# Neighbour quantiles over 16 graphs: the 21-slot end block sorted in mid-round, a later read-back, last finishes side by side, and the second round's tiles sorted entry by entry

## The chip, the cores and the metric

The kernel runs on one core of one Trainium2 chip. The metric is device microseconds of one execution. Timed runs of the kernel before, three of them, have a median of 7,337.73 us (7,328.73 to 7,385.34). One execution was also taken with the hardware profiler; it has its own time, which is given below.

## The reference

The input is a batch of B = 16 graphs ("entries") of N = 1024 nodes with C = 64 features, and a dense weighted adjacency that has about 16 neighbours in a row. Four layers follow each other, each with a residual and a layernorm. Layers 0 and 1 are dense products with the adjacency and small matrices. Layers 2 and 3 ("layer 0" and "layer 1" of the kernel's quantile part) drop some neighbours, and then take for each node and each feature a weighted sum of three quantiles over the neighbours that are left:

```python
adj_d = _dilate_adj(adj, mask)
# per node and feature: sort the valid neighbours' values, interpolate
sv = jnp.sort(jnp.where(valid[..., None], x[:, None, :, :], big), axis=2)
for tau, wt in zip((0.25, 0.5, 0.75), (0.25, 0.5, 0.25)):
    pos = jnp.clip(tau * (mf - 1.0), 0.0)
    lo, hi = floor(pos), ceil(pos)
    agg = agg + wt * (gather(lo) * (1.0 - frac) + gather(hi) * frac)
out = x + agg
y = relu(out @ W1 + b1) @ W2 + b2
x = _layernorm(x + y * mask)
```

The neighbour lists are the same in both quantile layers; the values are not.

## The kernel before

**Tiles and sizes.** The nodes of an entry are ordered by their number of neighbours and cut into NT = 8 tiles of 128. Tile t has lists of SIZES[t] slots (10, 11, 13, 14, 15, 17 and 19 for tiles 0 to 6). A slot of a tile is a [128, 64] fp32 block: one neighbour of each of 128 nodes. The eighth tile is split in two halves of 64 nodes, with 21 and 33 slots; the even and the odd entry of a pair put their halves into the same two blocks, so that each of the two end blocks (plans 7 and 8) is full. "Pair" means two entries that are sorted at once.

**Where the values come from.** Tiles 0 to 6 are gathered: `fetch_one` issues one indirect DMA per slot and entry on the GpSimd queue (L378), from a table in HBM into a ring `got_s` of ROOM = 60 slots by two entries. A tile takes SIZES[t] slots of the ring, and the slots come free when the tile that held them has been sorted and weighed. The end blocks are not gathered: `fill` picks their rows with matmuls. For each of slots 1 to 32 it builds a one-hot matrix `hot` from `place` (three of four on VectorE, one of four in two steps on ScalarE), runs 24 matmuls with it into PSUM (`pick`, L374), and after each four slots ScalarE copies them to the end blocks `got` (L780).

**Sorting and weighing.** `exchange` runs a pruned merge-exchange network on VectorE, with min and max between the tile and a scratch tile `other`. All VectorE work that is recorded through the `Metered` wrapper has line L211 in the profile. `weigh` then multiplies the wanted slots on ScalarE (L829 for tiles, L820 for end blocks) and adds them on VectorE into `agg`.

**Rounds.** The 16 rounds are quantile layer and pair: (0,0), (0,1), (1,0), (0,2), (1,1), ... (0,7), (1,6), (1,7). `sort_round(k)` starts the generator `fill(k)`, sorts tiles 6 down to 0 in turn, then waits until the fill is complete and sorts end block 7 (21 slots) and end block 8 (33 slots). In the very first round the two entries of the pair are sorted one after the other (`present` is (0,) and then (1,)); in all others both at once. After a round `finish` runs for its two entries: the small MLP, the layernorm, and 8 row scatters on the GpSimd queue (L888), to the table of the next layer or to the output. After the first quantile layer, `read_back` loads the table again (`x3`, L902 on the SP queue) and splits it into three bf16 parts for the picking matmuls of the second.

**What sets the order.** Nearly everything other than the sorts is a generator: `features` (layers 0 and 1, with `adj_r` loads, L433, on the SP queue), `lists` and `ordered` (which neighbours, and in which order), `fill`, `weigh`, `finish` and `read_back`. A planner, `Weave`, keeps a clock that adds up the estimated VectorE time of what was recorded; each `yield u` of a generator puts its next step u us later on that clock. After each exchange instruction `catch_up` records the steps that are due, and `fetch` issues the gathers for which the ring has room. `advance` and `finish` of the planner jump ahead when there is nothing else to do. VectorE, ScalarE and TensorE keep the recorded order; the GpSimd and SP queues are ordered by the scheduler. Each engine runs its queue in order, and waits for semaphores.

These lines carry the points that the change touches:

```python
for present in ((0,), (1,)) if k == 0 else ((0, 1),):
    tasks += [(k, t, present) for t in reversed(range(LISTED))]
...
weave.finish(filling)
for t in range(LISTED, NS):
    off = sum(SIZES[LISTED:t])
    got = tails[k][:, off : off + SIZES[t], :]
...
    exchange(t, (got, other[:, : SIZES[t], :]), cut)
    summed(t, got, None, (0, 1))
```

Of the kernel before, what the change touches and what calls it, by code (L numbers as in the profile page):

```python
# [26 lines left out]
LEAST = (1,) + SIZES[:7] + (20,)  # L27
# [189 lines left out]
def adj_resnorm_kernel(ctx: ExitStack, tc: tile.TileContext, x, adj_t, nodemask, w01, b01, w02, b02,  # L217
# [49 lines left out]
    def halves_of(b):  # L267

        return (7, 8) if b % 2 == 0 else (8, 7)
# [100 lines left out]
    def pick(dst, hot, parts, first=True):  # L370

        for c in range(NT):
            for q in range(3):
                nc.tensor.matmul(dst, hot[:, c, :], parts[:, c, q, :], start=first and c + q == 0,  # L374
                                 stop=c == NT - 1 and q == 2)
# [386 lines left out]
    def fill(k):  # L762

        while k and (k - 1, NS - 1) not in free:
            yield 1
        size, short = SIZES[NS - 1], SIZES[NS - 2]
        got = tails[k] = s.lists.tile([P, short + size, C], F32, name="got", tag="got_l", bufs=1)
        layer, both = members(k)
        for m, b, e in both:
            while e.parts[layer] is None or e.xs[layer] is None or e.place is None or e.none is None:  # L770
                yield 1
            at = [(rows, (0, short)[plan - LISTED], SIZES[plan]) for rows, plan in zip((lower, upper), halves_of(b))]
            for rows, off, _ in at:
                nc.scalar.copy(got[rows, off, :], e.xs[layer][rows, NT - 1, :])
            waiting = None

            def empty():
                for rows, off, most in at:
                    if waiting[0] < most:
                        nc.scalar.copy(got[rows, off + waiting[0] : off + waiting[0] + 4, :], waiting[1][rows])  # L780

            for i in range(1, size):
                if i % 4 == 1:
                    first, pg = i, pgs[i // 4 % 2]
                if i % 4 == 1:

                    far = s.work.tile([P, NT, P], F16, name="far", bufs=1)
                    nc.scalar.activation(far, e.place, AF.Abs, bias=minus_k[:, i + 2 : i + 3])
                    by_act = s.lists.tile([P, NT, P], BF, name="hot", bufs=HOTS)
                    nc.scalar.activation(by_act, far, AF.Relu, bias=one_f, scale=-1.0)  # L790
                if i % 4 == 3:
                    hot = by_act
                else:
                    hot = s.lists.tile([P, NT, P], BF, name="hot", bufs=HOTS)
                    dve.tensor_scalar(hot, e.place, float(i), None, op0=ALU.is_equal)
                whole = i < LEAST[NS - 2]
                if not whole:
                    nc.tensor.matmul(pg[:, i - first, :], e.none,
                                     ident_b[: KW - 1, i - 1 : i].to_broadcast([KW - 1, C]), start=True, stop=False)
                pick(pg[:, i - first, :], hot, e.parts[layer], whole)  # L800
                yield 2.4
                if i % 4 == 2 and waiting:
                    empty()
                if i % 4 == 0:
                    waiting = first, pg
            yield 5
            empty()
            yield 0.5
            e.filled[layer] = True

    def weigh(k, t, got, agg, which, present):

# [84 lines left out]
    def read_back(b, e, src):  # L897

        while b >= 2 and not entries[b - 2].filled[1]:
            yield 2  # L900
        x3 = s.feat.tile([P, NT, C], F32, name="x3", bufs=1)
        nc.sync.dma_start(x3, src[:N, :].rearrange("(t p) c -> p t c", p=P))  # L902
        yield 60
        parts = s.feat.tile([P, NT, 3, C], BF, name="x3p", bufs=2)
        yield from split(x3, parts, x3)
        e.parts[1] = parts
# [43 lines left out]
    tails = {}  # L950
# [5 lines left out]
    order_of_rounds += [(1, B // 2 - 2), (1, B // 2 - 1)]  # L956
    tasks = []
    for k in range(len(order_of_rounds)):
        for present in ((0,), (1,)) if k == 0 else ((0, 1),):
            tasks += [(k, t, present) for t in reversed(range(LISTED))]  # L960

    def prepare():
# [55 lines left out]
    def finish_round(k, agg, sums):  # L1018
        for gen in sums:
            while weave.runs(gen):  # L1020
                yield 1
        layer, both = members(k)
        if k == len(order_of_rounds) - 1:
            for m, b, e in both:
                weave.add(finish(b, e, layer, agg[:, m], m == 1))
            return
        for m, b, e in both:
            yield from finish(b, e, layer, agg[:, m])

    def exchange(t, pair, view):  # L1030

# [6 lines left out]
    def sort_round(k):  # L1038

        if k >= 2:  # L1040
            weave.finish(rounds[k - 2])
        filling = weave.add(fill(k), 4.0, 0.7 if k < 3 else 1.0)
        agg = s.feat.tile([P, 2, NT, C], F32, name="agg")
        sums = []

        def summed(t, got, which, present):
            if len(sums) >= 2:
                weave.finish(sums[-2])
            sums.append(weave.add(weigh(k, t, got, agg, which, present)))
            weave.catch_up()  # L1050

        for n, (_, t, present) in enumerate(tasks):
            if tasks[n][0] != k:
                continue
            fetch(n)
            got = gots[n]
            which = slice(present[0], present[-1] + 1)
            count = len(present)
            other = s.lists.tile([P, WIDE, C], F32, name="other", bufs=1)
            other = other[:, : count * SIZES[t], :].rearrange("p (e s) c -> p e s c", e=count)  # L1060
            exchange(t, (got[:, which], other), cut_pair)
# [319 lines left out]
```

## Time and profile before

| | |
|---|---|
| median of three timed runs | 7,337.73 us (7,328.73 to 7,385.34) |
| time of the profiled execution | 5,306.79 us |
| its span, first to last instruction | 5,304.9 us |
| mean granted TensorE clock | 0.743 |
| VectorE (DVE) busy | 4,297.6 us, 9,266 instructions |
| GpSimd (POOL) busy | 3,464.7 us, of it 3,170.9 in 2,944 gathers |
| TensorE (PE) busy | 3,435.2 us, 43,576 matmuls |
| ScalarE (ACT) busy | 2,809.1 us, 6,314 instructions |
| HBM traffic | 239.37 MB read, 12.59 MB written |

The profiled execution was 2,031 us shorter than the median of the timed runs. All durations of single instructions below are from the profiled execution. "Busy" is the time in which an engine executes; time in which its queue waits for a semaphore or spends on issuing is not in it. A wait is put down to what ended it: "DVE other <- DMA got_s" is time in which VectorE stood ahead of an instruction that writes `other`, until a gather into `got_s` had landed. The matmul durations overlap each other, so that the sum of their means is more than the busy time.

### The profile page before, as it was taken

The numbers are of one execution on the slowest core, as the hardware profiler recorded it, in microseconds if no ns is written. First come the engines' busy times: TensorE is split into PE (matmuls) and PEld (weight loads), VectorE is DVE, ScalarE is ACT, GpSimd is POOL, SyncE is SP. The second block draws the span as 40 slices with busy tenths as digits, with TensorE's granted clock in tenths as the row PEclk, the third lists the DMA queues.
The fourth block names the chain that finished last, engine by engine and source line by source line (L and its number), as shares of the span: only waits on it lengthen the run. The fifth ranks groups of instructions, "written<-read, shape, count | busy, mean of one in ns | idle before, by whom it ended". The sixth has DMA issues, their size and how long they took to land. (4 is left out here: it accounts for less than half of the span.)

```text
span 5304.9 us, 109613 instructions
## 1 busy us (share of the span) xinstructions
PE 3435.2 (65%) x43576; PEld 2659.3 (50%) x43576; DVE 4297.6 (81%) x9266; ACT 2809.1 (53%) x6314; POOL 3464.7 (65%) x3296
## 2 busy tenths in 40 slices
PE   6878886385775776666776785777769563424152
PEld 5756555264554565555565563655547352324141
DVE  2577849698788989797997988798999999596775
ACT  3466465456564665737384563738475653334242
POOL 0336417757567776767767574776767777777771
PEclk7888787687877787868787786878887775555555
DMA  2212212222222222222212122222222111111110
GB/s 84 76 50 69 68 32 66 47 48 54 48 60 52 59 61 57 57 55 45 73 41 58 46 52 53 57 59 50 60 50 58 25 28 26 25 24 27 26 24 7
DMA packets 420617, 259.31 MB, mean 49 GB/s; under 512 B 106602, under 2 KB 368890, under 8 KB 420090
## 3 DMA queue, kind: packets, MB, share of 16 engines
q0 software_dynamic: 102400, 105.06, 10.4%
q1 hardware_dynamic: 317690, 147.12, 9.7%
q8 instruction: 343, 5.62, 0.5%
q14 instruction: 184, 1.51, 0.1%
HBM read 239.37 MB, written 12.59 MB: 47 GB/s over the span
## 5 line engine op out<-in xcount | busy, mean ns | idle before, releaser
L378 POOL DMA_INDIRECT got_s<-table,idx x2944 | 3170.9, 1077 | 1650.7 <-issue 604.9
L374 PEld LDWEIGHTS <-hot 128*128 128x128 bf16 x24576 | 972.2, 109 | 1011.9 <-DVE hot L211 696.7
L374 PE MATMUL pgk<-x3p,hot 128*128 128x64 bf16 x12288 | 544.0, 211 | 460.8 <-DVE hot L211 396.6
L211 DVE TENSOR_TENSOR other<-got_s 128x512 f32<-128x512 f32 (+9 forms) x850 | 508.7, 609 | 387.4 <-DMA got_s<-table,idx 352.9
L374 PE MATMUL pgk<-x2p,hot 128*128 128x64 bf16 x12288 | 525.5, 208 | 320.4 <-DVE hot L211 261.6
L780 ACT COPY got<-pgk 64x256 f32<-64x256 f32 x416 | 151.6, 365 | 675.8 <-PE pgk L374 670.3
L536 PE MATMUL pr<-steps,near 128*128 128x512 bf16 x1536 | 415.1, 431 | 131.6 <-ACT junk L542 84.6
L211 DVE TENSOR_TENSOR got_s<-got_s 128x128 f32<-128x128 f32 (+9 forms) x867 | 482.0, 560 | 17.8
L481 PE MATMUL pa<-x,adj_r 128*128 128x65 f32 x2048 | 391.3, 375 | 133.7 <-ACT x L404 58.6
L628 PE MATMUL pk<-near,order 128*128 128x512 f16 x2048 | 468.0, 382 | 4.5 <-DVE order L211 4.2
L829 ACT ACTIVATE got_s<-got_s,wts 128x64 f32<-128x64 f32 x1568 | 396.5, 335 | 135.1 <-DVE got_s L211 128.9
L481 PEld LDWEIGHTS pa<-x,adj_r 128*128 128x128 f32 x2048 | 380.6, 289 | 141.7 <-ACT x L404 60.5
L211 DVE TENSOR_TENSOR got_s<-other 128x512 f32<-128x512 f32 (+9 forms) x731 | 402.2, 563 | 7.5
L211 DVE TENSOR_SCALAR hot<-place 128x1024 bf16<-128x1024 f16 x768 | 329.8, 435 | 60.1 <-PE pgk L374 60.0
L536 PEld LDWEIGHTS <-near 128*128 128x128 f16 x1536 | 162.2, 109 | 353.0 <-issue 228.4
L211 DVE TENSOR_TENSOR other<-other 128x384 f32<-128x384 f32 (+10 forms) x617 | 324.0, 525 | 17.3
L211 DVE MAX8 best<-code 128x8 f16<-128x1024 f16 x240 | 293.9, 1225 | 48.1 <-ACT code L639 43.0
L628 PEld LDWEIGHTS <-order 128*128 128x128 bf16 x2048 | 194.0, 98 | 233.6 <-issue 10.6
L542 ACT ACTIVATE junk<-pr,nb_st 128x1024 f16<-128x1024 f32 x256 | 281.7, 1105 | 36.7 <-PE pr L536 35.9
L580 PE MATMUL pv<-minus_n,takes 128*128 128x128 bf16 x1024 | 212.5, 241 | 133.1 <-DVE takes L211 132.6
L790 ACT ACTIVATE hot<-far,one_f 128x1024 bf16<-128x1024 f16 x256 | 294.0, 1148 | 8.6
L450 PE MATMUL px<-adj_r,x_s 128*64 128x128 f32 x2048 | 287.9, 302 | 13.6 <-ACT node_in L453 9.2
(205 smaller groups left out, 6748.9 us busy)
## 6 DMA issues: line engine op xcount, KB each, us to landing
adj_r<-in_adj_dram SPq DMA_DIRECT2D x256, 512.0 KB
got_s<-table,idx POOLq DMA_INDIRECT x2944
x_s<-in_x_dram SPq DMA_DIRECT2D x16, 256.0 KB
table<-x SPq DMA_DIRECT2D x16, 256.0 KB
x<-table SPq DMA_DIRECT2D x16, 256.0 KB
table<-x3s,rows POOLq DMA_INDIRECT x128
out_dram<-agg,out_rows POOLq DMA_INDIRECT x128
table<-no_row SPq DMA_DIRECT2D x12, 0.2 KB
```

The source lines that it names most:

```text
L211: return call(*args, **kwargs)
L374: nc.tensor.matmul(dst, hot[:, c, :], parts[:, c, q, :], start=first and c + q == 0, stop=c == NT - 1 and q == 2)
L378: nc.gpsimd.indirect_dma_start(out=dst, out_offset=None, in_=tab, in_offset=bass.IndirectOffsetOnAxis(ap=rows, axis=0))
L450: nc.tensor.matmul(px[C:, q * P : (q + 1) * P], x_s[:, jt, :], adj[t][:, jt, :], start=jt == 0, stop=jt == NT - 1)
L481: nc.tensor.matmul(pa[:, q, :], adj[i][:, jt, :], x1[:, jt, :], start=jt == 0, stop=jt == NT - 1)
L536: nc.tensor.matmul(pr[:, h * HALF : (h + 1) * HALF], near[:, c, t * P : (t + 1) * P], steps[:, ONSET + h * HALF - c * P :][:, :HALF], star ...
L542: nc.scalar.activation(junk, prs[t - 1], AF.Sign, bias=lim[:, i, t - 1 : t], scale=-1.0, accum_out=cut_at[:, i, t - 1 : t])
L580: nc.tensor.matmul(pv[:, cols], takes[:, c, rows], minus_n, start=False, stop=False)
L628: nc.tensor.matmul(cols, order[:, c, t * P : (t + 1) * P], left(c, slice(h * G, (h + 1) * G)), start=c == 0, stop=c == NT - 1)
L780: nc.scalar.copy(got[rows, off + waiting[0] : off + waiting[0] + 4, :], waiting[1][rows])
L790: nc.scalar.activation(by_act, far, AF.Relu, bias=one_f, scale=-1.0)
L829: nc.scalar.activation(got[:, m, i, :], got[:, m, slot_id, :], AF.Copy, scale=e.wts[:, t, i : i + 1])
```

## The change

`fill` makes two tiles in place of one, of 21 and of 33 slots, and fills in two passes: slots 1 to 20 for both entries, then slots 21 to 32 for both; `filled` notes that a pass is complete. From the third round on, the 21-slot block is sorted and weighed between tile 2 and tile 1 (`end(NS - 2)`), after the planner has recorded the first pass in full; the 33-slot block stays at the end. In the first two rounds both stay at the end. The second round's tiles are sorted one entry after the other, as those of the first were. `read_back` puts 60 us on the planner's clock ahead of its load for entries 0 to 11, and 40 instead of 60 behind it. `finish` of the two entries of a pair runs side by side in the last three rounds, where it did so in the last round alone; the second of the two uses other PSUM banks (`spare`).

```diff
@@ fill
-        size, short = SIZES[NS - 1], SIZES[NS - 2]
-        got = tails[k] = s.lists.tile([P, short + size, C], F32, name="got", tag="got_l", bufs=1)
+        middle, most = SIZES[NS - 2], SIZES[NS - 1]
+        ends = [s.lists.tile([P, size, C], F32, name="got", tag=f"got_{size}", bufs=1) for size in (middle, most)]
+        tails[k] = ends
         layer, both = members(k)
-        for m, b, e in both:
...
-            for i in range(1, size):
-                if i % 4 == 1:
-                    first, pg = i, pgs[i // 4 % 2]
...
-            e.filled[layer] = True
+        groups = 0
+        for low, high in ((1, middle), (middle, most)):
+            for m, b, e in both:
...
+                for i in range(low, high):
+                    if i % 4 == 1:
+                        first, pg = i, pgs[groups % 2]
+                        groups += 1
...
+                yield 5
+                empty()
+                yield 0.5
+                if high == most:
+                    e.filled[layer] = True
+            filled.add((k, low))
@@ read_back
         while b >= 2 and not entries[b - 2].filled[1]:
             yield 2
+        if b < B - 4:
+            yield 60
         x3 = s.feat.tile([P, NT, C], F32, name="x3", bufs=1)
         nc.sync.dma_start(x3, src[:N, :].rearrange("(t p) c -> p t c", p=P))
-        yield 60
+        yield 60 if b >= B - 4 else 40
@@ tasks
-        for present in ((0,), (1,)) if k == 0 else ((0, 1),):
+        for present in ((0,), (1,)) if k < 2 else ((0, 1),):
@@ finish_round
-        if k == len(order_of_rounds) - 1:
+        if k < order_of_rounds.index((0, B // 2 - 1)):
             for m, b, e in both:
-                weave.add(finish(b, e, layer, agg[:, m], m == 1))
-            return
-        for m, b, e in both:
-            yield from finish(b, e, layer, agg[:, m])
+                yield from finish(b, e, layer, agg[:, m])
+        else:
+            ends = [weave.add(finish(b, e, layer, agg[:, m], m == 1)) for m, b, e in both]
+            while any(weave.runs(gen) for gen in ends):
+                yield 1
@@ sort_round
+        def end(t):
+            got = tails[k][t - LISTED]
+            other = s.lists.tile([P, WIDE, C], F32, name="other", bufs=1)
+            exchange(t, (got, other[:, : SIZES[t], :]), cut)
+            summed(t, got, None, (0, 1))
+
         for n, (_, t, present) in enumerate(tasks):
             if tasks[n][0] != k:
                 continue
+            if t == 1 and len(present) == 2:
+                while (k, 1) not in filled:
+                    weave.advance()
+                end(NS - 2)
             fetch(n)
...
         weave.finish(filling)
-        for t in range(LISTED, NS):
-            off = sum(SIZES[LISTED:t])
-            got = tails[k][:, off : off + SIZES[t], :]
-            other = s.lists.tile([P, WIDE, C], F32, name="other", bufs=1)
-            exchange(t, (got, other[:, : SIZES[t], :]), cut)
-            summed(t, got, None, (0, 1))
+        if k < 2:
+            end(NS - 2)
+        end(NS - 1)
```

More of the change, by code (lines that the diff above doesn't have):

```diff
@@ L765, in fill @@
             yield 1
-        size, short = SIZES[NS - 1], SIZES[NS - 2]
-        got = tails[k] = s.lists.tile([P, short + size, C], F32, name="got", tag="got_l", bufs=1)
+        middle, most = SIZES[NS - 2], SIZES[NS - 1]
+        ends = [s.lists.tile([P, size, C], F32, name="got", tag=f"got_{size}", bufs=1) for size in (middle, most)]
+        tails[k] = ends
         layer, both = members(k)
-        for m, b, e in both:
[L770 to L780, printed above, removed]
-            for i in range(1, size):
-                if i % 4 == 1:
-                    first, pg = i, pgs[i // 4 % 2]
[L785 to L808, printed above, removed]
-            e.filled[layer] = True
@@ new lines, in fill, with empty @@
+        groups = 0
+        for low, high in ((1, middle), (middle, most)):
+            for m, b, e in both:
+                while e.parts[layer] is None or e.xs[layer] is None or e.place is None or e.none is None:
+                    yield 1
+                at = [(rows, ends[plan - LISTED], SIZES[plan]) for rows, plan in zip((lower, upper), halves_of(b))]
+                if low == 1:
+                    for rows, got, _ in at:
+                        nc.scalar.copy(got[rows, 0, :], e.xs[layer][rows, NT - 1, :])
+                waiting = None
+                def empty():
+                    for rows, got, size in at:
+                        if waiting[0] < size:
+                            nc.scalar.copy(got[rows, waiting[0] : waiting[0] + 4, :], waiting[1][rows])
+                for i in range(low, high):
+                    if i % 4 == 1:
+                        first, pg = i, pgs[groups % 2]
+                        groups += 1
+                        far = s.work.tile([P, NT, P], F16, name="far", bufs=1)
+                        nc.scalar.activation(far, e.place, AF.Abs, bias=minus_k[:, i + 2 : i + 3])
+                        by_act = s.lists.tile([P, NT, P], BF, name="hot", bufs=HOTS)
+                        nc.scalar.activation(by_act, far, AF.Relu, bias=one_f, scale=-1.0)
+                    if i % 4 == 3:
+                        hot = by_act
+                    else:
+                        hot = s.lists.tile([P, NT, P], BF, name="hot", bufs=HOTS)
+                        dve.tensor_scalar(hot, e.place, float(i), None, op0=ALU.is_equal)
+                    whole = i < LEAST[NS - 2]
+                    if not whole:
+                        nc.tensor.matmul(pg[:, i - first, :], e.none,
+                                         ident_b[: KW - 1, i - 1 : i].to_broadcast([KW - 1, C]), start=True, stop=False)
+                    pick(pg[:, i - first, :], hot, e.parts[layer], whole)
+                    yield 2.4
+                    if i % 4 == 2 and waiting:
+                        empty()
+                    if i % 4 == 0:
+                        waiting = first, pg
+                yield 5
+                empty()
+                yield 0.5
+                if high == most:
+                    e.filled[layer] = True
+            filled.add((k, low))
@@ L949, in adj_resnorm_kernel @@
     weave = Weave()
-    tails = {}
+    tails, filled = {}, set()
     free, gots, room, holders = set(), [], [0], [None] * ROOM
@@ L1022, in finish_round @@
         layer, both = members(k)
-        if k == len(order_of_rounds) - 1:
+        if k < order_of_rounds.index((0, B // 2 - 1)):
             for m, b, e in both:
-                weave.add(finish(b, e, layer, agg[:, m], m == 1))
-            return
-        for m, b, e in both:
-            yield from finish(b, e, layer, agg[:, m])
+                yield from finish(b, e, layer, agg[:, m])
+        else:
+            ends = [weave.add(finish(b, e, layer, agg[:, m], m == 1)) for m, b, e in both]
+            while any(weave.runs(gen) for gen in ends):
+                yield 1
     def exchange(t, pair, view):
```

## The prediction

> **What bounds the kernel now.** First the busy shares and the 40 slices of the page:
>
> ```profile
> PE 3435.2 (65%) x43576; PEld 2659.3 (50%) x43576; DVE 4297.6 (81%) x9266; ACT 2809.1 (53%) x6314; POOL 3464.7 (65%) x3296
> DVE  2577849698788989797997988798999999596775
> POOL 0336417757567776767767574776767777777771
> ```
>
> Two engines share the bound. VectorE (DVE) sorts; GpSimd (POOL) issues the 2,944 row gathers and 256 row scatters. POOL's digit 7 is nearly full: from 4,193 to 5,163 us it issued 696 DMAs in 970 us, 1.39 us each, of which only 1.08 is counted busy and the rest is "issue". So I read the idle time of both, by what ended it: the waits of DVE, then of POOL, then of SP and ACT.
>
> ```profile
> DVE other L211 <- DMA got_s<-table,idx: 352.9, 28, 26.4
> ...
> DVE near L211 <- DMA adj_r<-in_adj_dram: 36.0, 7, 22.6
> ```
> ```profile
> POOL got_s L378 <- DVE idx L211: 310.9, 8, 179.5
> POOL got_s L378 <- DVE other L211: 271.4, 103, 49.6
> ...
> POOL got_s L378 <- DVE y_x L211: 126.4, 3, 125.8
> ```
>
> DVE's great wait is for gathers. POOL's are for neighbour lists (`idx`, start-up) and for ring space (`other`: the sort of a tile must end before its slots are refilled). I then cut the span into rounds; a round begins where DVE starts on the 19-slot tile. Round 7 (2,642 to 2,955 us) shows the pattern:
>
> ```profile
> DVE other L211 <- DMA got_s<-table,idx: 29.2, 2, 24.9
> ...
> POOL got_s L378 <- DVE other L211: 30.6, 7, 28.8
> ```
> ```profile
> 2642.00:2955.00 313.00, 217.82 (x2805) 170.54 (x2805) 267.41 (x566) 175.26 (x402) 216.69 (x202) 0.75 0.22 53
> 4424.00:4699.00 275.00, 105.35 (x1620) 89.36 (x1620) 209.49 (x437) 96.12 (x251) 214.66 (x199) 0.55 0.13 26
> ```
>
> (Columns: window, then PE, PEld, DVE, ACT, POOL busy, clock, DMA.) While DVE sorts the two end blocks at the end of a round, POOL fills the 60-slot ring with the next round's first three tiles and stops (28.8 us). It resumes when the 19-slot tile is sorted, and later DVE stands still until the gathers of tile 1 have landed (24.9 us at 2,812). Both stalls belong to one loop: tail sorts late, ring refilled late, tile 1 late. In rounds 12 to 14 POOL no longer stops, and the round is as long as its 199 or so DMAs.
>
> **What the Trainium skill says.** "VectorE: DVE Perf Modes", section on the TRN2 errata, gives an fp32 tensor_tensor as (N+151)/0.96 ns: 691 ns for 512 elements. The trace has 690, and 286 for 128, so an added instruction costs about 0.15 us beside its elements. "SBUF — State Buffer", section "Who interferes with whom", says that a tensor_tensor with two SBUF inputs takes only a read interface from GpSimd and should not hold up descriptor generation. The trace agrees: a gather has a mean of 1.08 us both in round 7 (216.69/202, DVE 85% busy) and in round 13 (214.66/199, DVE 76% busy). So DVE work moved into a gather wait should not lengthen the wait. "Perfetto Trace Analysis", "Identifying Performance Opportunities", names repeated bubbles on the busiest engine as a sign of too few buffers; here the bubble is that of the ring, which the change leaves at 60 slots.
>
> **The change part by part**, against the profiled execution (5,306.8 us, span 5,304.9).
>
> *1. The 21-slot block moves from the round's end to ahead of tile 1 (rounds 2 to 15).* Its 49 instructions take 20 us: 1,315 to 1,336 in round 2, 5,189 to 5,208 in round 15; none is added. The wait just ahead of tile 1 was, from the timeline, 9.9, 11.8, 10.0, 14.7, 21.8, 24.9, 15.5, 18.0, 8.2 us in rounds 2 to 10 and none in rounds 11 and 12 (round 11 waits 9.1 us ahead of tile 2). The block covers at most 20 of each: 9.9+11.8+10.0+14.7+20+20+15.5+18.0+8.2 = 128 us. Above that stand two floors for rounds 3 to 11 (2,718 us together): DVE has 2,393 busy plus 18 per round of small gaps, 2,555; POOL has 1,797 DMAs at 1.39, 2,498. 2,718 less 118 (rounds 3 to 10) is 2,600, above both but near, so some of the wait will turn up elsewhere, as at tile 2. I take 105; bounds 0 and 128. In rounds 13 to 15 POOL is the limit, so their 142 us of DVE waits stay.
>
> *2. The fill in two passes that this needs.* Slots 1 to 20 of both entries, then 21 to 32 of both: the same 64 hots, 1,536 pairs of weight load and matmul and 26 copies per round, other order. The block's first instruction now waits for the last copy of pass one. Queued behind it on DVE are tile 1, tile 0, the hots of pass two, and so PE and POOL's ring. In the recorded order of after, pass one is complete 10 to 28 us of DVE work before the block in rounds 4 to 12, and just in time in rounds 13 to 15, where DVE waits for gathers anyway. Before, a tail recorded with no such lead (round 5) began without a wait. Cost taken: 0; if the lead is not enough, w us per round, priced below. The two tiles hold the same 54 slots, and the next fill still waits for the 33-slot block.
>
> *3. Last round.* POOL's last gather is at 5,154; tile 1 runs 5,147 to 5,162, tile 0 to 5,176, then finish work, the 21-slot block to 5,208, the 33-slot block to 5,244, `finish` and scatters to 5,305. With the block started at 5,144, tiles 1 and 0 end about 16 us later, at 5,192, the 33-slot sort at 5,228: 16 us gained; bounds 0 and 20.
>
> *4. Round 1 entry by entry.* 222 more DVE instructions: one entry's seven tiles cost 81 us (round 0), two at once 130 (round 1), so 162-130 = 32 us more. But POOL stands 125.8 us at 644 to 769 with the ring full and entry 3 not listed, and from 673 to 808 DVE has 55.7 busy of 135. Entry 2's remaining 44 gathers (44 x 1.29 = 57 us; 1.08 busy and 604.9/2,944 = 0.21 of issue each) and its 81 us of sorts fit there. After 808 DVE has 49 us less to sort and POOL 57 us less to issue. Part is lost to the in-round chain and to entry 5's list, for which POOL waits 42 us at 1,354: I take 35; bounds -32 and 57.
>
> *5. Read back later (entries 0 to 11).* The load `x<-table` is issued 60 us later and the split 40 later:
>
> ```profile
> SPq L902 <- DMA table<-x3s,rows: 1289.3, 15, 431.5
> ```
>
> SP stands in this load until the scatters have landed, with `adj_r` loads queued behind. This reached DVE once, 22.6 us at 3,241. I take 10; bounds 0 and 23. The later split is hidden by the round that lies between layer 1's write and its use (except pair 0, where it lands inside round 2).
>
> *6. `finish` side by side for rounds 13 and 14.* The same operations in parallel banks. Round 13's scatters for entries 14 and 15 come together rather than 70 us apart (4,857 and 4,953), but POOL was busy through that stretch: 0. Round 14's `finish` ends before the end counts: 0.
>
> Sum: 105+16+35+10 = 166 us, 3.1% of the profiled execution: 5,141.
>
> **From there to the timed runs.** Their median, 7,337.7, lies 2,031 us above the profiled execution, and no view shows where. I carry microseconds, not the ratio (which would give 7,108), because the gains are waits of fixed size: 7,337.7 - 166 = 7,172, said as 7,170. A measurement of this kernel can tell about 1% (73 us) from no change.
>
> **Rivals.**
> - *POOL alone is the bound in the timed runs.* If the 2,031 us are slower DMAs (2,031/3,200 = 0.63 us each), POOL never stops, and filling DVE's waits gains nothing. Left are parts 3 and 4: 51 to 73 us, 7,265 to 7,287, within 1%. For it: rounds 12 to 14 already look so. Against it: in the profile POOL stops in each of rounds 3 to 10. The same number results if the waits saved ahead of tile 1 reappear ahead of tile 2 or 0.
> - *The mid-round block waits for its fill: slower.*
>
> ```profile
> ACT got L780 <- PE pgk L374: 670.3, 148, 26.4
> ```
>
>   ACT stands up to 26.4 us for the picking matmuls before it can copy. At the end of a round this had long passed; mid-round DVE would stand w us in each of 14 rounds. The gain is gone at w = 166/14 = 12 us, 1% is lost from (166+73)/14 = 17 us, and 20 us would give 7,337.7+280-166 = 7,452. For it: if PE is what is slower in the timed runs, pass one is late. Against it: the mean of that wait is 4.5 us, and the lead is 10 to 28.
>
> **How the numbers follow.** Forecast 0.62, POOL alone or waits that only move 0.22, fill late 0.16. Prediction 7,170. The low end takes all upper bounds (128+20+57+23 = 228) with the ratio, 7,337.7 x (1-228/5,307) = 7,022, of which I keep 7,050; the high end reaches 50 us into the slower case, 7,390. The forecast's own range is 7,050 to 7,264. Faster by over 1%: 0.62; within 1%: 0.22; slower by over 1%: 0.16.
>
> **What would show it.** Right: DVE's wait for `got_s` falls by about 100 us and POOL's for `other` with it; rounds 4 to 10 shorten by 8 to 20 us; a 20 us run of `got` sorts stands ahead of tile 1; POOL's 125.8 us wait at 644 shrinks to about 70; after the last gather some 133 us remain instead of 150. Wrong: DVE waits for ACT `got` L780's copies at the block, round lengths unchanged with the waits now at tiles 2 and 0, or a profiled gain that the timed runs don't show.

## The result, and the profile after

The changed kernel takes 7,306.04 us (median of 20 timed runs, 7,271.8 to 7,324.09), the kernel before 7,331.09 us (median of 20, 7,301.86 to 7,385.34) beside it. The ratio is 0.9954, with a 95% interval from 0.9938 to 0.9970: 25 us between the medians, and 22 to 45 by the interval. The forecast was 166 us less. On the five chips of e1 to e17 (the "quick chips") the kernel before takes 5,294 to 5,307 us, on the chip of e18 (the "slow chip") 7,348 us, so times are compared only between runs of one chip, or as ratios to the kernel before.

By its span (5,304.9 us) the profile of before is an execution as on a quick chip, and the timed runs are all as on the slow one. On which chips they were made is not known. Only one set of experiments (e18) met the slow chip, so whether the slowness belongs to the chip or to its condition at that time is not shown. The profile of the changed kernel is of the slow kind: its span is 7,299.2 us. Its page:

```profile
PE 3976.7 (54%) x43576; PEld 2896.5 (40%) x43576; DVE 4336.7 (59%) x9509; ACT 2809.6 (38%) x6312; POOL 3320.8 (45%) x3296
...
DVE  2546535757556566465574856557484765647475
...
POOL 0432244444463553525445454546445353665652
```

DVE and POOL have their work of before (4,337 and 3,321 us), but hardly a slice is full. Neither bounds the kernel here. The waits of DVE (in us: total, times, longest):

```profile
DVE hot L211 <- remote: 657.8, 74, 27.3
DVE best L211 <- ACT code L639: 415.6, 24, 68.4
DVE hot L211 <- PE pgk L374: 259.4, 61, 39.6
DVE y_m L211 <- PE pd L884: 175.7, 17, 37.4
DVE other L211 <- ACT got L784: 155.6, 7, 55.3
...
DVE other L211 <- DMA got_s<-table,idx: 12.6, 4, 6.2
```

The wait for gathers, 352.9 us before, is 12.6. DVE now stands for what PE makes: free one-hot buffers (`hot`; "remote" is a releaser that the profile can't name), counts of the lists (`best`, after PE's `pk`), the MLP (`y_m`). And it stands 155.6 us for the fill's copies ahead of the end blocks, all in rounds 12 to 15: 106.5 ahead of the mid-round block (32.4, 55.3 and 18.4 in rounds 13, 14 and 15), the rest ahead of the 33-slot block. The waits over all engines show where PE itself stands:

```profile
PEld L374 <- issue: 1934.1, 1498, 31.6
POOL got_s L378 <- DVE other L211: 1181.2, 87, 119.7
ACT got L784 <- PE pgk L374: 1029.7, 116, 36.2
```

PE's weight loads for the picks wait 1,934 us for nothing that the profile shows. In the profile of before the same wait was:

```profile
PEld L374 <- issue: 260.6, 212, 6.2
```

POOL's wait for ring space had 271.4 us there, ACT's for picks 670.3. The timeline shows what the issue time is (start, duration, engine, line, operation; in brackets the idle time before it):

```profile
464.69 0.94 POOL L378 DMA_INDIRECT got_s<-table,idx  x1 [0.30 <-issue]
465.36 0.10 PEld L374 LDWEIGHTS <-order 128*128 128x128 bf16 x1 [2.00 <-issue]
465.93 0.95 POOL L378 DMA_INDIRECT got_s<-table,idx  x1 [0.30 <-issue]
466.75 0.21 PE L374 MATMUL ordered_x<-x2p,order 128*128 128x64 bf16 x1 [2.59 <-issue]
467.19 0.95 POOL L378 DMA_INDIRECT got_s<-table,idx  x1 [0.30 <-issue]
468.15 0.10 PEld L374 LDWEIGHTS <-order 128*128 128x128 bf16 x1 [2.69 <-issue]
```

PE needs 0.1 us for the weights and starts one instruction in 1.4 us (465.36, 466.75, 468.15), while POOL issues a gather each 1.25 us, undisturbed. Elsewhere the steps are 0.70. Two such stretches by windows (window, then PE, PEld, DVE, ACT, POOL busy with instructions, clock, DMA share, GB/s):

```profile
441.40:504.60 63.20, 7.68 (x52) 4.32 (x52) 3.65 (x5) 0.00 (x0) 42.08 (x45) 0.53 0.12 24
...
3553.40:3626.40 73.00, 17.62 (x68) 5.85 (x66) 12.53 (x22) 2.10 (x9) 49.66 (x52) 0.53 0.13 24
```

In the first, 63 us, PE makes 52 matmuls, DVE 5 instructions and POOL 45 gathers. The same PE instructions on a quick chip (trace of e5, the same kernel):

```profile
368.70:370.20 1.50, 1.50 (x58) 1.50 (x55) 1.42 (x3) 0.00 (x0) 1.20 (x2) 1.00 0.18 42
...
2498.90:2504.90 6.00, 6.00 (x74) 3.25 (x70) 5.83 (x9) 2.92 (x10) 4.64 (x5) 1.00 0.14 30
```

1.5 us in place of 63, and 6 in place of 73. I call a stretch slow when it holds at least five weight loads close together that start over 0.55 us after the one before. The trace of 7,299 us has 118 of them, 2,027 us in all; the same instructions take some 360 us in e5's. The difference is nearly 1,670 of the 2,110 us between the two spans. The exact counts depend on how near to each other late loads must be.

### The profile page after: what moved, and what is told of

Its sections match the earlier page's. It is cut to its first block, busy times and chain, and to the rows that moved or that the text cites. A ratio compares the mean times of both kernels' runs of the same rounds, so it can differ in the third digit from the quotient of the medians.

```text
span 7299.2 us, 109906 instructions
## 1 busy us (share of the span) xinstructions
PE 3976.7 (54%) x43576; PEld 2896.5 (40%) x43576; DVE 4336.7 (59%) x9509; ACT 2809.6 (38%) x6312; POOL 3320.8 (45%) x3296
## 4 chain that ended last, share of the span: by engine, by line
PE 29%; DVE 24%; issue 20%; another core or an unknown queue 13%; ACT 12%; POOL 1%; DMA 0%; DVEq 0%; ACTq 0%; POOLq 0%
PE pgk L374 10%; DVE other L211 8%; PE pk L628 5%; DVE got_s L211 5%; DVE got L211 4%; PE px L450 3%; PE pr L536 2%; PE pa L481 2%; ACT got_s L835 2%; DVE best L211 2%; ACT junk L542 2%; PE ordered_x L374 2%; ACT dist L557 1%; ACT got L784 1%
## 5 line engine op out<-in xcount | busy, mean ns | idle before, releaser
L378 POOL DMA_INDIRECT got_s<-table,idx x2944 | 3035.6, 1031 | 3510.5 <-DVE other L211 1181.2
L374 PEld LDWEIGHTS <-hot 128*128 128x128 bf16 x24576 | 1100.5, 112 | 2039.9 <-issue 1646.0
L374 PE MATMUL pgk<-x3p,hot 128*128 128x64 bf16 x12288 | 646.4, 214 | 758.2 <-issue 409.7
L374 PE MATMUL pgk<-x2p,hot 128*128 128x64 bf16 x12288 | 666.6, 216 | 643.2 <-issue 429.3
L628 PE MATMUL pk<-near,order 128*128 128x512 f16 x2048 | 537.8, 412 | 107.1 <-issue 100.3
L211 DVE TENSOR_TENSOR other<-got_s 128x512 f32<-128x512 f32 (+8 forms) x900 | 515.7, 584 | 55.3 <-ACT got_s L1018 25.6
L211 DVE TENSOR_TENSOR got_s<-got_s 128x256 f32<-128x256 f32 (+8 forms) x918 | 490.7, 538 | 66.0 <-ACT got_s L835 39.9
L211 DVE TENSOR_TENSOR other<-other 128x128 f32<-128x128 f32 (+11 forms) x642 | 327.3, 510 | 22.9 <-remote 3.4
L802 PE MATMUL pgk<-ident_b,none 32*128 32x64 bf16 x448 | 93.0, 208 | 441.7 <-ACT got L784 369.2
L450 PEld LDWEIGHTS px<-adj_r,x_s 128*64 128x64 f32 x2048 | 273.7, 161 | 118.3 <-issue 95.0
```

The source lines that it names most:

```text
L211: return call(*args, **kwargs)
L378: nc.gpsimd.indirect_dma_start(out=dst, out_offset=None, in_=tab, in_offset=bass.IndirectOffsetOnAxis(ap=rows, axis=0))
L450: nc.tensor.matmul(px[C:, q * P : (q + 1) * P], x_s[:, jt, :], adj[t][:, jt, :], start=jt == 0, stop=jt == NT - 1)
L628: nc.tensor.matmul(cols, order[:, c, t * P : (t + 1) * P], left(c, slice(h * G, (h + 1) * G)), start=c == 0, stop=c == NT - 1)
L802: nc.tensor.matmul(pg[:, i - first, :], e.none, ident_b[: KW - 1, i - 1 : i].to_broadcast([KW - 1, C]), start=True, stop=False)
```

## The experiments

**Is a second trace of the kernel before slow too, and is PE or POOL the bound?** e1 is the kernel before, unchanged. e2 and e3 leave out two of the three bf16 parts of each pick, in the changed kernel and in the kernel before:

```diff
-            for q in range(3):
+            for q in range(1):
                 nc.tensor.matmul(dst, hot[:, c, :], parts[:, c, q, :], start=first and c + q == 0,
```

e4 puts plain loads on SP's queue in place of the gathers, so that the sorts get other rows:

```diff
-                gather(got[:, m, i, :], table[layer][b % TABLES], e.idx[:, LINKS[t] + i - 1 : LINKS[t] + i])
+                nc.sync.dma_start(got[:, m, i, :], table[layer][b % TABLES][i % NT * P : i % NT * P + P, :])
```

> The kernel before, unchanged, to see a second trace of it. The one trace of it lasts 5,305 us and its timed runs 7,331; the trace of the changed kernel lasts 7,299, as its timed runs do, and holds 82 stretches (1,731 us in all) in which PE starts an instruction only every 0.7 us or more. Theory (PE's instruction stream is slow in the timed runs and sets their time): a trace of the kernel before that lasts about 7,330 us shows the same stretches, some 1,700 us of them, and PE's weight loads at L374 wait about 1,900 us for 'issue' in place of 261. Rival (POOL alone is the bound in the timed runs): POOL's gathers come out longer (about 0.6 us each) and its queue hardly stops. A trace of 5,305 us again would tell nothing new.

> The changed kernel with one of the three bf16 parts in each pick, so that two thirds of the 24,576 picking matmuls and their weight loads are left out (the values lose their low bits). Sorts, gathers, copies and one-hots are the same. Theory (PE's instruction stream is the bound): 16,384 of 43,576 pairs go, of which the slow stretches take their share, so 800 to 1,500 us less than 7,306. Rival (POOL alone is the bound): within 100 us of 7,306, since POOL's work is the same.

> The same for the kernel before: one of three bf16 parts in each pick. Theory (the sum of the prediction was right for a chip whose PE keeps up, and the slow PE stream hid it): this falls by 800 to 1,500 us too, and e2 is then faster than this one by 80 to 170 us, where the full kernels differ by 25 to 34. Rival (the parts of the change bring only the 25 us or so whatever bounds the kernel): e2 and e3 differ by under 50 us.

> The changed kernel with each of the 2,944 row gathers of POOL replaced by a plain load of 128 rows in sequence from the same table, on SP's queue (the sorts get other rows; the bytes and rows moved are the same). POOL is left with its 256 scatters. Theory (PE's instruction stream is slow of itself): the slow stretches of PE stay, and the time falls by less than 500 us. Rival A (POOL alone is the bound): the time falls by over 1,500 us while PE's slow stretches play no part in it. Rival B (PE's stream is slow because POOL's gathers run beside it): the slow stretches go with the gathers, PE's wait for 'issue' at L374 falls from 1,934 us to under 400, and the time falls by over 1,500 us.

Measured: e1 5,299.88 us, e2 5,112.54, e3 5,255.27, e4 4,913.53, the kernel before 5,297.51. All four ran on a quick chip, so none of the 800 to 1,500 us could be found there, and e1's trace has no slow stretch. The theories on the 7,300 us stay untested by them. What they do tell: with light picks the change is worth 143 us (5,255 - 5,113), as the theory expected of a PE that keeps up. e2 had a mean TensorE clock of 0.678, and e3 of 0.670 like the slow execution's 0.670: a mean granted clock as low as that goes with 5,255 us too, though e2 and e3 have fewer matmuls.

**What is the change worth on a quick chip, and which part brings it?** e5 is the changed kernel. e6 has parts 1 to 3 alone (block and two-pass fill), e7 all but the mid-round block, e8 the kernel before with round 1 entry by entry:

```diff
-        for present in ((0,), (1,)) if k == 0 else ((0, 1),):
+        for present in ((0,), (1,)) if k < 2 else ((0, 1),):
```

> The changed kernel, unchanged, beside the kernel before on one chip. A second trace of the kernel before lasts 5,293 us with timed runs of 5,298, and has no slow stretch of PE. Theory (the prediction's sum holds where PE's stream keeps up, and slow stretches of PE hid it in the first comparison): where the kernel before takes about 5,300 us, this takes 5,130 to 5,200 and no stretch of slow PE is in its trace; where the kernel before takes about 7,330 us, this takes 7,300 and PE is slow in some 1,700 us of it. Rival (the change itself makes PE slow): 7,300 us beside 5,300 us of the kernel before. Rival (the change is worth 25 us anywhere): 5,270 us beside 5,300.

> The mid-round 21-slot block and the two-pass fill alone (parts 1 to 3 of the prediction); round 1, the read-back and the finishes as in the kernel before. Prediction's parts: 105 + 16 = 121 us less than the kernel before (bounds 0 and 148). Rival (the waits move to tiles 2 and 0 or to the fill): within 30 us of the kernel before. Where the kernel before takes about 7,330 us: within 40 us of it, by either.

> The changed kernel with the 21-slot block put back to the end of every round (the fill stays in two passes; round 1 entry by entry, the later read-back and the side-by-side finishes stay). Prediction's parts 4 to 6: 45 us less than the kernel before (bounds -32 and 80). Rival (the gain is not in the mid-round block): as fast as the whole change. Where the kernel before takes about 7,330 us: within 40 us of it.

> The kernel before with one change: round 1's tiles sorted entry by entry. Prediction's part 4: 35 us less than the kernel before (bounds -32 and 57), from POOL's 125.8 us wait at 644 us falling to about 70. Rival (the 222 added instructions cost their 32 us): 0 to 32 us more than the kernel before. Where the kernel before takes about 7,330 us: within 40 us of it.

| kernel | us | against before (5,294.95) | ratio, 95% interval |
|---|---|---|---|
| e5, whole change | 5,188.83 | -106 | 0.9798 (0.9782 to 0.9814) |
| e6, mid-round block and fill | 5,117.20 | -178 | 0.9662 (0.9645 to 0.9678) |
| e7, all but the block | 5,265.85 | -29 | 0.9940 (0.9923 to 0.9956) |
| e8, round 1 entry by entry | 5,378.73 | +84 | 1.0154 (1.0137 to 1.0171) |

The change itself doesn't make PE slow: e5's trace has no slow stretch. Its gain on a quick chip needs the block: without it, in e7, 29 us are left of 106, so the block is worth 77 us on top of the other parts. The block and the two-pass fill together bring 178. How much of that the fill brings alone was not timed on a quick chip (its run, e18, fell on the slow one). It may be much: e7 without its fill would be parts 4 to 6, and these, run as e8 and e10, lose 84 and gain 13 us. DVE's wait for gathers in e1 and then in e6:

```profile
DVE other L211 <- DMA got_s<-table,idx: 357.6, 27, 26.4
...
DVE near L211 <- DMA adj_r<-in_adj_dram: 36.0, 7, 22.5
```
```profile
DVE other L211 <- DMA got_s<-table,idx: 175.7, 16, 28.9
```

182 us less, for 178 us of time. e6's round 7 takes 287 us, of which DVE works 269, where the kernel before took 313; and POOL hardly stops for ring space (30.6 us in all before, 5.2 now):

```profile
2532.00:2819.00 287.00, 213.27 (x2774) 170.47 (x2781) 269.30 (x568) 174.11 (x399) 224.23 (x203) 0.79 0.24 60
```
```profile
POOL got_s L378 <- DVE other L211: 5.2, 13, 1.5
```

Round 1 entry by entry lost. These are e8's round 1 (DVE, window 661 to 1,070), and POOL from 600 us to the start of round 3 in e1 and then in e8:

```profile
DVE other L211 <- DMA got_s<-table,idx: 44.6, 2, 36.8
DVE other L211 <- issue: 21.9, 1, 21.9
```
```profile
POOL got_s L378 <- DVE y_x L211: 124.1, 2, 123.8
...
POOL got_s L378 <- DVE idx L211: 40.2, 1, 40.2
...
POOL got_s L378 <- DVE other L211: 15.9, 13, 12.3
```
```profile
POOL got_s L378 <- DVE other L211: 125.9, 23, 53.9
...
POOL got_s L378 <- DVE idx L211: 70.2, 1, 70.2
```

POOL's great wait went, as forecast, and came back as a wait for ring space (15.9 to 125.9) and for the next lists (40.2 to 70.2). Entry 2's seven sorts lasted some 170 us from 661, because the steps of the lists are recorded between them. Then DVE stood 66.5 us ahead of entry 3's tiles: 44.6 for gathers, and 21.9 (the "issue" line) ahead of an instruction that reads gathered slots, for a cause that the profile doesn't name. Starts of rounds (first exchange of tile 6, us in the traces) and the end of DVE:

| kernel | round 2 | 3 | 5 | 8 | 11 | 13 | end |
|---|---|---|---|---|---|---|---|
| e1, before | 1,062 | 1,434 | 2,022 | 2,943 | 3,871 | 4,414 | 5,267 |
| e8, round 1 alone | 1,070 | 1,465 | 2,055 | 2,964 | 3,945 | 4,509 | 5,352 |
| e6, block and fill | 1,049 | 1,406 | 1,965 | 2,819 | 3,689 | 4,250 | 5,090 |
| e9, without round 1 | 1,049 | 1,396 | 1,961 | 2,832 | 3,735 | 4,297 | 5,125 |
| e5, whole change | 1,061 | 1,446 | 1,999 | 2,872 | 3,771 | 4,333 | 5,162 |

By the start of round 3 e8 is 31 us late, which is about its added work; at round 8 it is 21 late. The other 60 or so of its 84 us are lost in rounds 8 to 11, where DVE waits longer for adjacency loads, gathers and one-hots than in e1. Why an early round should cost that much later is not shown. In the whole change (e5 beside e9) nothing more is lost after round 3.

**What do the later read-back and the side-by-side finishes do?** e9 is the changed kernel with round 1 as before, e10 the kernel before with parts 5 and 6 alone, and e16 is e6 with the finishes side by side:

```diff
-        if k < len(order_of_rounds) - 1:
+        if k < order_of_rounds.index((0, B // 2 - 1)):
```

> The changed kernel with one part undone: round 1's tiles are again sorted for both entries at once. Alone, that part cost 84 us (5,379 beside 5,295), and the mid-round block alone took 5,117 where the whole change took 5,189, 72 us apart. Theory (the entry-by-entry round is what costs the 72 us, the later read-back and the side-by-side finishes are worth next to nothing): 5,105 to 5,130 us where the kernel before takes 5,297. Rival (the later read-back or the finishes cost it): 5,160 or more. Where the kernel before takes about 7,330 us: 7,250 to 7,330, as the whole change.

> The kernel before with the later read-back and the side-by-side finishes of rounds 13 and 14 alone (parts 5 and 6 of the prediction). Prediction: 10 us less than the kernel before, bounds 0 and 23. The change without the mid-round block took 29 us less than the kernel before, and round 1 alone 84 more: if parts add up, these two parts and the two-pass fill are worth 113 us where the block stays at the end. Theory (they matter when the round is long): 60 to 120 us less. Rival (the two-pass fill is what is worth it): 0 to 25 us less. Where the kernel before takes about 7,330 us: within 40 us of it.

> The mid-round block, the two-pass fill and the side-by-side finishes of rounds 13 and 14; round 1 and the read-back as in the kernel before. The block alone took 5,117 us; block, finishes and later read-back 5,156. Theory (the later read-back costs it: the picks come late and in a heap ahead of the MLP's matmuls in PE's queue, and DVE's `y_m` waits for pd rise to 59.8 us; the finishes save some 10 us in rounds 13 to 15): 5,100 to 5,120 us. Rival (the finishes cost it): 5,140 or more. Where the kernel before takes about 7,330 us: within 60 us of it.

e9 took 5,155.75 us (ratio 0.9739, 0.9723 to 0.9755), e10 5,281.15 (0.9968, 0.9957 to 0.9979), e16 5,109.07 (0.9645, 0.9629 to 0.9661). My theory for e9 was wrong: 39 us of the 72 between e5 and e6 are not round 1's. e16, which came out as its theory had it, puts them on the read-back: with the block in mid-round it costs some 47 us (5,156 - 5,109), where with the finishes, and the block at the end, it saves 13. The side-by-side finishes show no effect clear of the intervals (e16 is 8 us below e6, on another chip). In e9 DVE waits for gathers and for PE's MLP:

```profile
DVE other L211 <- DMA got_s<-table,idx: 210.2, 19, 28.6
DVE y_m L211 <- PE pd L884: 59.8, 12, 20.4
```

In e6 these are 175.7 and 18.0 us; in e16, which differs from e9 in the read-back alone, 193.8 and 17.7. So the rise in the wait for the MLP goes with the later read-back. That picks which can only start later stand in one heap ahead of the MLP's matmuls in PE's queue is argued from these lists, not tested. Of the kernels that do the whole work, e16 has the lowest time, 187 us under the kernel before on a quick chip, not clear of e6. Neither has run on the slow chip.

**Does a late PE alone take the gain away?** e11 to e13 make three more copies of each pick ahead of the real one; e14 and e15 make 26 more of every thirteenth:

```diff
+                    for _ in range(3):
+                        pick(pg[:, i - first, :], hot, e.parts[layer])
                     if not whole:
```
```diff
+                    picks[0] += 1
+                    for _ in range(26 if picks[0] % 13 == 0 else 0):
+                        pick(pg[:, i - first, :], hot, e.parts[layer])
                     if not whole:
```

> The kernel before with each pick preceded by three more copies of its 24 matmuls into the same PSUM bank, which the real ones then overwrite: 73,728 more pairs of weight load and matmul, at a mean of 37 ns between matmuls of e1 some 2,730 us more for PE, and nothing else. PE was busy 3,391 us of 5,293, so it becomes the bound: 6,100 to 7,500 us, with DVE waiting for PE (`hot` for pgk, `y_m` for pd) over 500 us in place of 89.

> The changed kernel with the same three extra copies of each pick. Theory (a late PE takes the gain away: the round is then as long as PE's work, and the mid-round block waits for its fill): within 60 us of e11, and DVE waits for ACT's copies into `got` ahead of the 21-slot block, over 50 us in all, as in the trace of 7,299 us. Rival (a late PE leaves the gain as it is): 90 us or more faster than e11, no wait at the block.

> The mid-round block and two-pass fill alone, with the same three extra copies of each pick. Where PE kept up it was the fastest, 72 us ahead of the whole change. Theory (PE bound: orders of DVE's work hardly count): within 60 us of e11 and e12. Rival (the parts keep their worth): 70 us faster than e12.

> The kernel before with 26 extra copies of every thirteenth pick ahead of it (78 bursts of some 23 us in PE's queue, 1,800 us in all; the real pick overwrites what they leave). In the trace of 7,299 us there are 82 slow stretches, 21 us on average. Where PE has no slack, 7,100 us; since part of the bursts falls where PE would have waited anyway, 5,900 to 6,900 us.

> The changed kernel with the same bursts. Theory (PE that stands still for some 20 us at a time takes the gain away, because the fill is then late for the mid-round block): within 60 us of e14, and DVE waits for the copies into `got` ahead of the block over 50 us in all. Rival (stretches do it no more than an even load did): 90 us or more faster than e14, no such wait.

Measured: e11 6,464.22, e12 6,325.55, e13 6,302.06; e14 6,186.63, e15 6,079.93. The gain is 139 us under the even load and 107 under the bursts. Both theories fell: more work for PE, even or in heaps, does not take the gain away. The lead of the block and fill alone over the whole change shrinks from 72 to 23 us (e13 beside e12). The wait for the fill's copies came, 57.3 us in e12 and 37.5 in e15, of which 9.3 and 24 stood at the mid-round block and the rest at the 33-slot block, and the gain bore it. DVE's waits in e11 and then in e12 show one thing more:

```profile
DVE hot L211 <- PE pgk L374: 782.5, 270, 12.1
...
DVE other L211 <- DMA got_s<-table,idx: 37.5, 6, 15.2
```
```profile
DVE hot L211 <- PE pgk L374: 554.9, 206, 11.1
...
DVE other L211 <- DMA got_s<-table,idx: 44.1, 5, 15.5
```

In e11, too, there is next to no wait for gathers to fill (37.5 us, none of it in rounds 2 to 12), and yet the change gains 139 us: DVE waits 228 us less for PE to free its one-hot buffers. So the change can pay in another way than the one it was priced by.

**What stands beside the slow stretches?** That led back to the trace of 7,299 us. Each of its 82 slow stretches (by a stricter count, with at least eight late starts) lies beside gathers; POOL is about half to four fifths busy in every one. Take as a run all gathers and scatters that start within 0.7 us of the end of the last, and as a late start a PE instruction (matmul or weight load) that is followed by the next only after 0.55 to 2.3 us. Inside the runs 2,043 of 38,126 PE starts are late (5.4%), outside 437 of 49,151 (0.9%). On a quick chip (e5) it is 296 of 76,115 inside (0.4%). The rates say the same. On the slow chip the runs cover 58% of the span and hold 44% of PE's starts, 9 in a microsecond beside 16 outside. In e5 they cover 85% and hold 87%, 17 in a microsecond beside 15. Late starts are thickest where DVE hardly works: in slots of 5 us with DVE under 10% busy, 928 of 3,953 starts inside runs are late on the slow chip, and 1 of 837 in e5. It may be that the slowness feeds itself, since a DVE that stands still leaves POOL free to gather; but DVE also stands still because PE is late, so the counts don't show which comes first.

Three other causes are unlikely. Instruction fetch: the Trainium skill ("Runtime: NRT & Kernel Launch", Instruction fetch mechanics) says that each engine's instructions come in blocks of 16 KiB, ahead of their use. The trace agrees: 343 packets of 16 KiB on one queue, with a median of 1.10 us in the profile of before and 1.04 in that of after, and the late starts are spread about evenly between two fetches. Slower gathers: their mean is 1,031 ns, less than the 1,077 (3,170.9 us / 2,944) of the profile before. The granted clock: it was 0.53 in both slow stretches above, but also in this window of e5, with 190 matmuls in 51 us:

```profile
4000.00:4051.00 51.00, 32.09 (x190) 26.06 (x192) 49.02 (x116) 12.05 (x51) 40.33 (x36) 0.53 0.25 65
```

**What is the change worth without gathers?** e17 puts e4's plain loads into the kernel before.

> The kernel before with each of POOL's 2,944 row gathers replaced by a plain load of 128 rows in sequence on SP's queue, as e4 did with the changed kernel (4,914 us; DVE then sorts other rows). Theory (the change is worth what it takes out of DVE's waits for gathers): without gathers there is nothing to fill, and this takes 4,860 to 4,960, within 60 us of e4, the 32 us of the entry-by-entry round on its side. Rival (the order of the blocks is worth something of itself): 5,000 or more. Where the kernel before takes about 7,330 us, the same 4,900, if the gathers are what slows PE.

e17 took 4,947.51 us, e4 4,913.53. Their ratios to the kernel before, 0.9358 (0.9330 to 0.9386) and 0.9266 (0.9245 to 0.9287), differ by 0.9%, some 49 us; the medians by 34. e17 came within 60 us of e4, as its theory had it. The gain of 106 us shrinks to a third or a half of it when there is no wait for gathers to fill. It doesn't vanish.

**The two-pass fill alone, and the slow chip.** e18 is e6 with the block put back to the end of every round:

```diff
-            if t == 1 and k >= 2:
-                while (k, 1) not in filled:
-                    weave.advance()
-                end(NS - 2)
...
-        if k < 2:
-            end(NS - 2)
+        end(NS - 2)
```

> The kernel before with the two-pass fill alone: slots 1 to 20 of both entries, then 21 to 32 of both, into two tiles; both end blocks stay at the end of the round. The prediction took 0 for it. If parts add up, it is worth 100 us (5,195). Rival (the parts depend on each other, round 1's cost above all): within 40 us of 5,297. Where the kernel before takes about 7,330 us: within 40 us of it.

This one fell on the slow chip: 7,396.44 us beside 7,348.32 of the kernel before, ratio 1.0078 (1.0052 to 1.0104), 48 us more and so a little outside the 40 that were expected. It is the nearest thing to a trace of the kernel before on such a chip, since only the order of the fill differs. It has 96 slow stretches (2,069 us) by the count that gave 82, and late starts are 6.2% inside gather runs (2,305 of 37,382) and 0.9% outside (470 of 49,895). Its waits of DVE:

```profile
DVE hot L211 <- remote: 669.7, 78, 46.1
DVE hot L211 <- PE pgk L374: 442.5, 82, 42.1
DVE best L211 <- ACT code L639: 263.6, 19, 66.7
...
DVE other L211 <- DMA got_s<-table,idx: 10.0, 2, 9.2
```

The last line answers a part of the main question. With the block at the end of the round, where it was before, DVE waits 10 us for gathers on the slow chip, none of it from round 2 on, and 352.9 and 357.6 in the two traces on quick chips (the profile of before, and e1). The wait that the change was priced by isn't there: DVE is held up by PE, POOL has filled the ring meanwhile, and then waits 1,109.6 us for DVE. It does not answer why the gain is only 25 us, since e11 has no such wait either and e12 gains 139. What can be read from the two lists of the slow chip is where the waits went. From e18 to the changed kernel DVE's waits for `hot` fall from 1,112 to 917 us, as they do from e11 to e12; but those for the lists' counts (`best`) rise from 264 to 416, and those for the fill's copies come up from none to 155.6. Why they rise there, and not in e12 to that extent, was not tested.

## Why the prediction was wrong, by its own steps

**From there to the timed runs** is the step that failed. It said "no view shows where" the other 2,031 us are, and carried the 166 us over as "waits of fixed size". Its own list of signs had this one, "a profiled gain that the timed runs don't show". The profile before and the timed runs were executions that behave differently, and the bound of one was used for the other. On the slow chip the wait for gathers, the wait "of fixed size" that part 1 lives by, has 10.0 us (e18) and 12.6 (the changed kernel) in place of 352.9. DVE stands there for what PE makes. The change moved those waits about: 155.6 us for its fill came up (e18's list has none at a block), others fell, and 25 us were left. That the wait which was priced is missing is shown; that this alone took the gain away is not, for e11 lacks it too and e12 gains 139 us. The loss against a quick chip's 106 us is thus explained in part.

**Part 1** (105 us with bounds 0 and 128) had the right mechanism on a quick chip. Parts 1 to 3 together brought 178 us where 121 were forecast (e6). Rounds 2 to 10 became 169 us shorter (1,062 to 3,871 before, 1,049 to 3,689 in e6, less the 13 of the start). In these rounds DVE's wait for gathers fell from 162 to 38 us, 125 less and within the ceiling of 128; the rest left other waits, among them 22.5 us for adjacency loads and 10 for `hot`, which part 1 had not counted. In rounds 13 to 15, whose waits were to stay, the gather line fell from 145 to 89 us, but 35 us of waits with no releaser named stand there instead, and the rounds became only some 13 us shorter.

One reading under part 1 was wrong. The prediction compared gathers of rounds 7 and 13 and found that DVE's work does not lengthen them; but DVE is busy for most of both. In the same profile the gathers that have `tensor_tensor` work beside them for over 80% of their time take 1.12 us on average (1,604 of them), those beside `MAX8` 0.95 (135), and those that have DVE work beside them for under 10% take 0.94 (344). So the trace does not agree with what was taken from the Trainium skill there: sorts beside gathers do cost, 0.18 us a gather. Beside the waits this is small.

**Part 2** at 0: on a quick chip the fill is not late (in e6 DVE doesn't wait ahead of the mid-round block), but what the fill is worth alone was not timed there. On the slow chip the fill in two passes costs 48 us by itself, which no step had. Why is open.

**Part 3** (16 us) did not show: from round 15's start to the end DVE took 285.9 us in e1 and 284.2 in e6.

**Part 4** (35 us gained) has the wrong sign: 84 us lost alone, 33 on top of the rest (5,189 - 5,156). The 32 us of added work were right: DVE's busy time from 220 us to round 3 is 979.8 in e8 and 946.0 in e1. Wrong was the cover: "81 us of sorts fit there" left out the lists' steps between the sorts (some 170 us in all), and ring space, which took over from the wait that went. That accounts for the 31 us at round 3; the rest of e8's 84 is open.

**Part 5** (10 us, with part 6 at 0) was right alone, 13 us (e10), and wrong in the sum: on top of the block the later read-back costs some 47 us. "Hidden by the round that lies between" had looked at the data's arrival, and not at DVE's wait for the MLP, which rose from 17.7 to 59.8 us.

On a quick chip these come to 106 us for 166. **Rival A** named within 1%, and 7,265 to 7,287; the measured 7,306 is within 1%, but by luck, for its reason was wrong: gathers were no slower, and POOL was 45% busy. **Rival B**'s mechanism, a fill that is late because PE is, is there on the slow chip (106.5 us at the block, where 280 were priced), and not on a quick one. The high end, 7,390, was said to reach into the slower case; it is 52 us over 7,337.7 and so inside the 1% (73 us), and the slower case lay outside the range.

Open: what in the chip holds PE back beside gathers. Plain loads on the slow chip would test whether the gathers are the cause or only the company; that has not run. Nor is it shown where the 25 us come from that the change does gain there, on top of the 48 us that its fill costs; the block and fill alone (e6) have not run there.

## What to carry to other kernels

Before pricing a change from a profile, see that its span agrees with the timed runs. If it doesn't, the waits it shows may not exist where the time is taken; a trace that lasts as long as the timed runs comes first. And price the parts of a change together: the later read-back saved 13 us with the finishes where the block stood at the end, and cost 47 once it had moved.

## What the hardware showed that I had not expected

One program on two chips took 5,294 and 7,348 us, each steady within 1% or so. On the slow one TensorE started instructions 0.70 us apart, or at multiples of it, for up to 73 us beside GpSimd's row gathers. And 73,728 more pairs of weight load and matmul cost 1,165 us (e11), 16 ns each, while TensorE's busy time rose by 1,864 us (3,391 in e1, 5,255 in e11): over a third of the added work found room in its idle time. And `tensor_tensor` work beside a gather makes the gather longer, 1.12 us where it takes 0.94 without.
